# A graph network on one core: SyncE fetches single rows beside GpSimd's gathers

## The chip, the cores and the metric

The kernel runs on one core of a Trainium2 chip. The metric is the device time of one execution in microseconds (us); the median of ten runs stands for the kernel. One execution was also recorded by the hardware profiler, and its trace gives the start and duration of each instruction on TensorE (PE, with its weight loads as PEld), VectorE (DVE), ScalarE (ACT), GpSimd (POOL) and SyncE (SP). What only a sequencer does, such as issuing a DMA, is listed under the engine's name with a q (SPq) and is not counted as busy.

## The reference

Two layers of message passing over a graph of 12,500 nodes with 32 features and 200,000 edges. The edges are sorted by target.

```
h = relu(layernorm(x))
x = x + (sum over edges of h[src] / norms, by dst) @ W + b          # first layer
h = relu(layernorm(x))
# second layer: i = dst, j = src
msg = concat(h[i], h[j] - h[i])                                     # 64 values for each edge
m = relu(relu(relu(msg @ W1 + b1) @ W2 + b2) @ W3 + b3) @ W4 + b4
x = x + (sum of m by dst) / max(count, 1)
```

The product with W1 is split by nodes: one table, tab_i, holds what a target adds to the first hidden layer, and another, tab_j, what a source adds. Both have a row for each node. tab_j is float32 with 64 values (256 bytes) a row, and row number + 48 belongs to a node (OFF = 48).

## The kernel before

A tile is 128 edges, a chunk is 4 tiles (TPC), and a pair is two chunks, 1,024 edges. There are 391 chunks and 196 pairs (NPAIR). The first part of the kernel, up to about 1260 us, computes degrees and the first layer and writes tab_i and tab_j to DRAM, block by block. The last blocks of tab_j and tab_i are written at about 1275 us.

The second layer is one loop over the pairs, written out in full with a schedule by hand: each engine executes its instructions in the order in which the loop issues them. In iteration m of the loop stand

- gather_in(m): the source rows of pair m. For each of the eight tiles GpSimd issues one indirect DMA (helper gather, line 210) that reads 128 row numbers from src_j in SBUF and fetches 128 rows of tab_j into the tile gj. gj has six buffers.
- prepare(m + 3): SyncE issues two DMAs, ai (the rows of tab_i for the pair's targets, line 1003, five buffers) and row (each edge's target relative to its window, spread over the partitions, line 1006, four buffers).
- the stages of earlier pairs, on TensorE with ScalarE and VectorE behind it: fourth(m-6), flip(m-5), third(m-4), second(m-3), first(m-1). first (lines 1022 to 1039) transposes gj into PSUM and adds the product of ai with a one-hot matrix; second and third are the products with W2 and W3 (1047, 1059); flip transposes back (1068), and VectorE copies the result to SBUF (1070); fourth sums messages by target (1079).
- turn(m + 1): VectorE makes the one-hot matrix turned from row (line 1012).

A tiny product with ident_b at the start of first (line 1027) is where TensorE waits for the gathers of a pair. At the end of the program SyncE and the other engines load one flag (bad_i, line 1138) into a register, and a fallback runs only if it is set; here it is not.

Each DMA that SyncE issues signals one of eight semaphores in turn, and waits that the DMA eight before it, which had the same semaphore, has landed.

Of the kernel before, what the change touches and what calls it, by code (L numbers as in the profile page):

```python
# [8 lines left out]
F32 = mybir.dt.float32  # L9
# [7 lines left out]
P = 128  # L17
# [3 lines left out]
HID = 64  # L21
# [4 lines left out]
OFF = 48  # L26
# [5 lines left out]
NPAD = NBLK * P  # L32

TPC = 4
CHUNK = TPC * P
NCH = -(-N_EDGES // CHUNK)
NTR = -(-N_EDGES // P)
# [46 lines left out]
DPAD = (DIR + NDG * GD) * CHUNK  # L84

PC = 32

NROW = NPAD + P

# [2 lines left out]
def gnn_kernel(  # L92
# [20 lines left out]
    nc = tc.nc  # L113
# [17 lines left out]
    tab_j = dram.tile([NPAD, HID], F32, name="tab_j")  # L131
# [9 lines left out]
    def parts(rows):  # L141

        return rows.rearrange("(p j) c -> p j c", p=NPART)
# [25 lines left out]
    xp = fp.tile([NPART, P, D], F32, name="xp")  # L169
    pieces = [slice(j, j + PC) for j in range(0, P, PC)]  # L170
    for at in pieces:
# [37 lines left out]
    def gather(tile_ap, table, col):  # L209
        nc.gpsimd.indirect_dma_start(  # L210
            out=tile_ap, out_offset=None, in_=table,
            in_offset=bass.IndirectOffsetOnAxis(ap=col, axis=0))
# [9 lines left out]
    o = 1 + D  # L222
# [32 lines left out]
    for i, at in enumerate(pieces):  # L255
        h, a = hx[:, at, :D], xp[:, at, :]
        m = fp.tile([NPART, PC], F32, name="la_m", bufs=2)
        nc.vector.tensor_reduce(m, a, AX.X, OP.add)
        nc.vector.tensor_scalar(m, m, 1.0 / D, None, op0=OP.mult)
        nc.vector.tensor_sub(h, a, m[:, :, None].to_broadcast([NPART, PC, D]))  # L260
        nc.vector.tensor_mul(a, h, h)
        v = fp.tile([NPART, PC], F32, name="la_v", bufs=2)
        nc.vector.tensor_reduce(v, a, AX.X, OP.add)
        nc.vector.tensor_scalar(v, v, 1.0 / D, EPS, op0=OP.mult, op1=OP.add)
        sd = fp.tile([NPART, PC], F32, name="la_sd", bufs=2)
        nc.scalar.activation(sd, v, AF.Sqrt)
        nc.vector.reciprocal(v, sd)
        nc.vector.scalar_tensor_tensor(
            h, h, 0.0, v[:, :, None].to_broadcast([NPART, PC, D]), op0=OP.max, op1=OP.mult)
        nc.sync.dma_start(parts(tab_h[OFF:, :])[:, at, :], hx[:, at, :])  # L270
# [2 lines left out]
    first.close()  # L273
    src_j = stay.tile([P, NT], I32, name="src_j")

    def gather_chunk(rows, table, g):
        for t in range(min(TPC, NTR - g * TPC)):
            c = g * TPC + t
            gather(rows[:, t, :], table, src_j[:, c : c + 1])

# [4 lines left out]
    o = dst.offset + DIR * CHUNK  # L285
# [8 lines left out]
    with tc.tile_pool(name="deg", bufs=3) as hp, tc.tile_pool(  # L294
        name="deg_ps", bufs=1, space=bass.MemoryType.PSUM
# [164 lines left out]
        for m, b in enumerate(batches):  # L460
# [4 lines left out]
            if to > gathered:  # L465
                c = slice(gathered * TPC, to * TPC)
                nc.vector.tensor_scalar(src_j[:, c], src_i[:, c], OFF, None, op0=OP.add)
                for g in range(gathered, to):
                    rows = early.tile([P, TPC, D + 1], F32, name="rows_early", bufs=6)
# [9 lines left out]
            for t in range(b, end):  # L479
                g, i = divmod(t - b, HT)  # L480
# [197 lines left out]
    def advance(running):  # L678

        for r in list(running):  # L680
            if next(r, running) is running:
                running.remove(r)
# [7 lines left out]
    NPAIR = -(-NCH // 2)  # L690
    live = {}

    def halves(m):
        return [k for k in range(2) if 2 * m + k < NCH]
# [4 lines left out]
    with tc.tile_pool(name="e0", bufs=8) as sp, tc.tile_pool(name="nu", bufs=1) as np_, tc.tile_pool(  # L699
        name="direct", bufs=1) as dp, tc.tile_pool(name="e0_ps", bufs=1, space=bass.MemoryType.PSUM) as pp, tc.tile_pool(  # L700
        name="nu_ps", bufs=1, space=bass.MemoryType.PSUM) as np_ps:
# [119 lines left out]
        table = dp.tile([P, PART * D3 + P - D3], BF16, name="table")  # L821
# [94 lines left out]
        for m in range(EARLY, DIR + LAG + 1):  # L916
            if m < DIR:
                rows_of[m] = sp.tile([P, TPC, D3], BF16, name="rows")
                gather_chunk(rows_of[m], tab_hn[:, :], m)
# [12 lines left out]
            for slot in slots:  # L932
# [7 lines left out]
                if slot % LATER == 0:  # L940
                    advance(running)
                    later, r = divmod(slot // LATER, NEXT)
# [19 lines left out]
    with tc.manual_schedule(), tc.tile_pool(name="prep", bufs=3) as prep, tc.tile_pool(name="e1", bufs=3) as ep, tc.tile_pool(name="fn", bufs=2) as fp, tc.tile_pool(  # L962
        name="p1_ps", bufs=2, space=bass.MemoryType.PSUM
# [8 lines left out]
        def finish_nodes(q):  # L972

            n = min(J, NBLK - J * q)
            at = slice(J * q, J * q + n)
            c = fp.tile([P, J], F32, name="fn_c")[:, :n]
            nc.vector.tensor_scalar(c, cnt[:, at], 1.0, None, op0=OP.max)
            r = fp.tile([P, J], F32, name="fn_r")[:, :n]
            nc.vector.reciprocal(r, c)
            some = fp.tile([P, J], F32, name="fn_some")[:, :n]  # L980
            nc.vector.tensor_scalar(some, cnt[:, at], 1.0, None, op0=OP.min)
            z = fp.tile([P, J, D], F32, name="fn_z")[:, :n]
            nc.vector.tensor_mul(
                z, b4s[:, None, :].to_broadcast([P, n, D]), some[:, :, None].to_broadcast([P, n, D]))
            nc.vector.tensor_add(z, z, x1[:, at, :])
            yield
            po = message[:, :n]
            for j in range(n):
                nc.tensor.matmul(po[:, j, :], sums.block(J * q + j), w4s, start=True, stop=True)  # L989
            yield  # L990
            y = fp.tile([P, J, D], F32, name="fn_y")[:, :n]
            nc.vector.tensor_mul(y, po, r[:, :, None].to_broadcast([P, n, D]))  # L992
            nc.vector.tensor_add(y, y, z)
            r0 = P * J * q
            nc.sync.dma_start(blocks(out[r0 : r0 + P * n, :]), y)

        def prepare(m):

            v = live[m] = {}
            n, g = len(halves(m)), 2 * m  # L1000
            ai = v["ai"] = prep.tile([P, 2, 3 * HID], BF16, name="ai", bufs=5)
            w = 3 * HID
            nc.sync.dma_start(ai[:, :n], bass.AP(
                tensor=tab_i.tensor, offset=tab_i.offset + STEP * g * w, ap=[[w, P], [STEP * w, n], [1, w]]))
            row = v["row"] = prep.tile([P, 2, CHUNK], F16, name="row", bufs=4)
            nc.sync.dma_start(row[:, :n], bass.AP(
                tensor=rel_row.tensor, offset=rel_row.offset + g * CHUNK, ap=[[0, P], [CHUNK, n], [1, CHUNK]]))

        def turn(m):
            v, n = live[m], len(halves(m))  # L1010
            turned = v["turned"] = prep.tile([P, 2, CHUNK], BF16, name="turned", bufs=3)
            nc.vector.tensor_scalar(turned[:, :n], v["row"][:, :n], part_s, None, op0=OP.is_equal)

        def gather_in(m):
            gj = live[m]["gj"] = ep.tile([P, TPC, 2, HID], F32, name="gj", bufs=6)
            if len(halves(m)) < 2 or (2 * m + 2) * TPC > NTR:
                nc.vector.memset(gj, 0.0)
            for k in halves(m):
                g = 2 * m + k
                gather_chunk(gj[:, :, k, :], tab_j[:, :], g)  # L1020

        def first(m):
            v = live[m]
# [72 lines left out]
        for m in range(AHEAD + 1):  # L1096
            prepare(m)
        turn(0)

        LAST = NPAIR - 1  # L1100
        ENDING = 22
        SHORTER = {second: (12,), third: (20, 10), flip: (18, 8), fourth: (21, 14, 7)}
# [4 lines left out]
        for m in range(NPAIR):  # L1107
            for stage, lag in zip(stages, (1, 3, 4, 5, 6)):
                lag -= len([back for back in SHORTER.get(stage, ()) if LAST - m < back])
                todo[m + lag].append((m, stage))  # L1110
        for now in todo[LAST - ENDING :]:
            now.sort(key=lambda job: (rank(job[1]), job[0]))
        todo[LAST + 1 :] = [[
            (LAST - 2, flip), (LAST - 1, second), (LAST, first), (LAST - 1, third), (LAST - 2, fourth), (LAST, second),
            (LAST - 1, flip), (LAST, third), (LAST - 1, fourth), (LAST, flip), (LAST, fourth)]]
        for m, now in enumerate(todo):
            if m < NPAIR:
                gather_in(m)
            if m == 0:
                for lane in ending:  # L1120
                    assert next(lane, lane) is lane
            if m == LAST:
                ready[NQ - 1] = finish_nodes(NQ - 1)
                next(ready[NQ - 1])
            if m + AHEAD + 1 < NPAIR:
                prepare(m + AHEAD + 1)
            advance(running)
            for k, stage in now:
                stage(k)
                if stage is fourth and (k % (GRP // 2) == GRP // 2 - 1 or k == LAST):  # L1130
                    add_messages(k // (GRP // 2))
            if m + 1 < NPAIR:
                turn(m + 1)
# [5 lines left out]
    with tc.If(bad > 0):  # L1139
        sums0 = dram.tile([NROW, D + 1], F32, name="sums0")  # L1140
        sums1 = dram.tile([NROW, D], F32, name="sums1")
        with tc.tile_pool(name="gp", bufs=1) as gp, tc.tile_pool(name="ge", bufs=1) as ge, tc.tile_pool(
            name="ge_ps", bufs=1, space=bass.MemoryType.PSUM
# [11 lines left out]
            spare = gp.tile([P, 1], F32, name="spare")  # L1155
# [37 lines left out]
            with tc.For_i(0, NTR, 1) as i:  # L1193
                s, d, same, r = edges(i)
                rows = ge.tile([P, D3], BF16, name="g_rows")
# [12 lines left out]
            for q in range(NQ):  # L1208
                n = min(J, NBLK - J * q)
                part = ge.tile([P, J, D + 1], F32, name="g_part")  # L1210
# [9 lines left out]
            with tc.For_i(0, NTR, 1) as i:  # L1220
                s, d, same, r = edges(i)
                gi = ge.tile([P, 3 * HID], BF16, name="g_gi")
                gather(gi, tab_i[:, :], d)
                gj = ge.tile([P, HID], F32, name="g_gj")
# [29 lines left out]
            c = gp.tile([P, NBLK], F32, name="g_c")  # L1254
# [39 lines left out]
```

## Time and profile before

| | |
|---|---|
| median of 10 runs | 3263.04 us (3261.81 to 3267.4) |
| the profiled execution's own time | 3262.19 us |
| its span in the profile | 3260.3 us |
| GpSimd busy | 2443.2 us (75%), of which gathers of gj 1484.6 us (1,563 instructions) |
| TensorE busy | 2539.5 us (78%) |
| VectorE, ScalarE busy | 1554.9 us (48%), 1531.6 us (47%) |
| first and last row of the second layer's gathers | 1277.0 and 3232.7 us |
| granted clock of TensorE | 0.867 on average, 0.82 in the second layer (2000 to 2500 us) |

The span runs from the first to the last instruction that the profiler saw; the device time holds some 1.9 us more. The second layer takes the last three fifths of the span. In rows of instruction groups the numbers after the bar are the busy time in us and the mean of one instruction in ns, and after the second bar the engine's idle time just before these instructions, with what ended it.

### The profile page before, as it was taken

What the parts mean: (1) busy time and instruction counts of PE and PEld (TensorE: products, weight loads), DVE (VectorE), ACT (ScalarE), POOL (GpSimd) and SP (SyncE); (2) the same over time, 40 slices, a digit from 0 to 9 for tenths busy, and PEclk for the clock granted to TensorE, in tenths of its full rate; (3) what the DMA queues carried; (4) which work ended last, traced back from release to release, by engine and by line L of the source; (5) the groups of instructions that cost most, each with busy time, mean ns of one, the idle gap of its engine ahead of it and who ended that gap; (6) DMA issues with size and microseconds to landing.
All of it is one profiled execution on the core that took longest, in us unless ns stands there. A gap on an engine that the chain in (4) does not pass through costs nothing. (4 is left out here: it accounts for less than half of the span.)

```text
span 3260.3 us, 45387 instructions
## 1 busy us (share of the span) xinstructions
PE 2539.5 (78%) x15791; PEld 1614.6 (50%) x15791; DVE 1554.9 (48%) x4067; ACT 1531.6 (47%) x3647; POOL 2443.2 (75%) x2529
## 2 busy tenths in 40 slices
PE   3777999889998995777777777777777777777776
PEld 2664667666666774344434444444444444444333
DVE  8997877777777874222222222222222222222233
ACT  4887888788887882222222222222222222222232
POOL 7777777777776775777777777777777777777775
PEclk8688999999999996788888888888888888888998
DMA  5114121111121112222222222222222222222221
GB/s 110 33 28 94 28 40 35 34 39 33 38 41 36 33 34 66 63 63 63 63 63 63 66 65 63 63 63 63 63 63 63 66 62 65 63 63 63 63 66 31
DMA packets 242764, 180.29 MB, mean 55 GB/s; under 512 B 155496, under 2 KB 191016, under 8 KB 242528
## 3 DMA queue, kind: packets, MB, share of 16 engines
q0 software_dynamic: 80224, 73.28, 12.5%
q1 hardware_dynamic: 157436, 100.80, 11.3%
q10 hardware_dynamic: 4868, 3.23, 0.6%
q8 instruction: 128, 2.10, 0.3%
q14 instruction: 108, 0.88, 0.1%
HBM read 159.32 MB, written 17.78 MB: 54 GB/s over the span
## 5 line engine op out<-in xcount | busy, mean ns | idle before, releaser
L210 POOL DMA_INDIRECT gj<-tab_j,src_j x1563 | 1484.6, 950 | 495.0 <-issue 416.0
L210 POOL DMA_INDIRECT rows<-tab_hn,src_j x752 | 760.9, 1012 | 238.3 <-issue 161.5
L901 ACT ACTIVATE count<-count 128x396 bf16<-128x396 f32 x1857 | 772.9, 513 | 117.2 <-PE count L899 110.2
L899 PE MATMUL count<-oh,lo 128*128 128x396 bf16 x1857 | 483.9, 333 | 68.8 <-DMA rows_early<-tab_h,src_j 24.4
L1079 PE MATMUL ps<-hot,h 128*128 128x256 f32 x1566 | 533.1, 499 | 1.8 <-ACT acc L660 1.2
L1070 DVE COPY h<-p 128x512 f32<-128x512 f32 x196 | 135.4, 691 | 795.5 <-PE p L1068 793.2
L1079 PEld LDWEIGHTS ps<-hot,h 128*128 128x128 f32 x1566 | 379.0, 255 | 183.0 <-issue 104.1
L1038 ACT ACTIVATE h<-p 128x512 f32<-128x512 f32 x196 | 117.0, 597 | 680.7 <-PE p L1034 680.7
L1027 PE MATMUL p<-gj,ident_b 128*1 128x8 bf16 x196 | 34.2, 174 | 486.0 <-DMA gj<-tab_j,src_j 470.9
L845 PE MATMUL st<-count,table 128*128 128x192 bf16 (+1 forms) x3822 | 393.1, 246 | 2.8 <-DVE acc_d L658 2.7
L845 PEld LDWEIGHTS <-table 128*128 128x128 bf16 x3822 | 321.0, 98 | 66.4 <-issue 24.5
L835 DVE TENSOR_SCALAR oh<-number,key 128x1176 bf16<-128x1176 f16 x619 | 318.4, 535 | 70.6 <-PE count L899 69.3
L1061 ACT ACTIVATE h3t<-p,b3c 128x512 f32<-128x512 f32 x196 | 134.7, 687 | 422.2 <-PE p L1059 422.1
L662 DVE TENSOR_TENSOR acc<-acc,ps 64x64 f32<-64x64 f32 (+1 forms) x198 | 44.7, 226 | 603.7 <-PE ps L1079 563.3
L1027 PEld LDWEIGHTS <-ident_b 128*1 128x1 bf16 x196 | 15.5, 79 | 632.8 <-issue 632.5
L1049 ACT ACTIVATE h<-p,b2s 128x1024 f32<-128x1024 f32 x196 | 217.8, 1111 | 118.4 <-PE p L1047 118.4
L686 DVE TENSOR_TENSOR hot<-rel_h,kept 128x512 f32<-128x512 f16 x391 | 250.0, 681 | 2.3
L899 PEld LDWEIGHTS <-lo 128*128 128x128 bf16 x1857 | 174.5, 99 | 152.8 <-issue 100.2
L1034 PE MATMUL p<-turned,ai 128*64 128x512 bf16 x1173 | 235.1, 524 | 0.0
L1047 PE MATMUL p<-h,w2s 64*128 64x512 f32 x782 | 226.1, 654 | 1.3 <-ACT h L1049 1.3
L1059 PE MATMUL p<-h,w3s 128*64 128x512 f32 x782 | 220.1, 641 | 1.8 <-ACT h3t L1061 1.6
L210 POOL DMA_INDIRECT rows_early<-tab_h,src_j x160 | 156.4, 977 | 48.8 <-issue 40.8
(256 smaller groups left out, 2861.8 us busy)
## 6 DMA issues: line engine op xcount, KB each, us to landing
row<-rel_row SPq DMA_DIRECT2D x195, 256.0 KB
gj<-tab_j,src_j POOLq DMA_INDIRECT x1563
ai<-tab_i SPq DMA_DIRECT2D x195, 96.0 KB
rows<-tab_hn,src_j POOLq DMA_INDIRECT x752
srow<-hi_row SPq DMA_DIRECT2D x48, 98.0 KB
tab_i<-nu_terms SPq DMA_DIRECT2D x23, 192.0 KB
rows_back<-tab_early SPq DMA_DIRECT2D x48, 66.0 KB
tab_j<-nu_aij SPq DMA_DIRECT2D x23, 128.0 KB
```

The source lines that it names most:

```text
L210: nc.gpsimd.indirect_dma_start(out=tile_ap, out_offset=None, in_=table, in_offset=bass.IndirectOffsetOnAxis(ap=col, axis=0))
L686: nc.vector.tensor_tensor(hot, rel_h[:, g * TPC : (g + 1) * TPC][:, :, None].to_broadcast([P, TPC, W]), lanes_f[:, None, :W].to_broadcast( ...
L835: nc.vector.tensor_scalar(oh, column, key[:, i : i + 1], None, op0=OP.is_equal)
L845: nc.tensor.matmul(ps[:, : tiles * WD], table[:, h * D3 : h * D3 + P], c[:, :tiles, h, :], start=(h == 0), stop=(h == PART - 1))
L899: nc.tensor.matmul(ps[:, :w], lo[:, i % TPC // 2, :, i % 2], oh[:, a * WD : b * WD], start=True, stop=True)
L901: nc.scalar.activation(counts[g][:, t, a:b, :].rearrange("p h d -> p (h d)"), ps[:, :w], AF.Copy)
L1034: nc.tensor.matmul(p1[k * HID : (k + 1) * HID].rearrange("p t e -> p (t e)"), v["ai"][:, k, i * HID : (i + 1) * HID], v["turned"][:, k], s ...
L1047: nc.tensor.matmul(p2[:, k], w2s[s, :], v["h1"][s, :], start=True, stop=True)
L1049: nc.scalar.activation(h2[:, :n], p2[:, :n], AF.Relu, bias=b2s)
L1059: nc.tensor.matmul(p3[k * HID : (k + 1) * HID], w3s, v["h2"][:, k], start=True, stop=True)
L1070: nc.vector.tensor_copy(h3[:, :, :rows], p4[:, :, :rows])
L1079: nc.tensor.matmul(both[: n * HID, :n, o : o + W], v["h3"][:, t, : n * HID], v["hot"][:, t, :n], start=(i == 0 and t == 0), stop=(last and ...
```

## The change

In the second layer one tile of every eighth pair, 23 tiles in all, is no longer gathered by GpSimd. SyncE fetches its 128 rows one by one into a tile of its own, spare, and VectorE copies that into gj. The rows are spread over the eight iterations ahead of the pair: in each of them SyncE loads 16 source numbers from DRAM into its registers and issues 16 DMAs of one row each, whose source addresses it computes from the registers. This happens in iterations 0 to 183, right after prepare. The last tile of the pair's second chunk is the one that moves. GpSimd has 1,540 gathers of gj instead of 1,563; SyncE has 2,944 more DMAs, 2,944 register instructions for their addresses, and 368 loads into registers (184 for the address of src, 184 for 16 numbers each) with 184 additions; VectorE has 23 more copies, each of which waits for the last eight row fetches.

```diff
+ROWS = 16
+EVERY = P // ROWS
...
-    def gather_chunk(rows, table, g):
-        for t in range(min(TPC, NTR - g * TPC)):
+    def gather_chunk(rows, table, g, n=TPC):
+        for t in range(min(n, NTR - g * TPC)):
             c = g * TPC + t
             gather(rows[:, t, :], table, src_j[:, c : c + 1])
...
         def prepare(m):
 
-            v = live[m] = {}
+            v = live.setdefault(m, {})
...
             for k in halves(m):
                 g = 2 * m + k
-                gather_chunk(gj[:, :, k, :], tab_j[:, :], g)
+                gather_chunk(gj[:, :, k, :], tab_j[:, :], g, TPC - (k == 1 and m in fetched))
+            if m in fetched:
+                nc.vector.tensor_copy(gj[:, TPC - 1, 1, :], live[m].pop("spare"))
+
+        def fetch_rows(m, part):
+
+            v = live.setdefault(m, {})
+            if part == 0:
+                v["spare"] = prep.tile([P, HID], F32, name="spare", bufs=2)
+            o = ((2 * m + 2) * TPC - 1) * P + part * ROWS
+            _, numbers = nc.values_load_multi_w_load_instructions(
+                src[o : o + ROWS].rearrange("(o c) -> o c", o=1), [mybir.EngineType.SP], min_val=0,
+                max_val=NPAD - OFF - 1, skip_runtime_bounds_check_because="numbers of nodes")
+            for k, number in enumerate(numbers):
+                r = part * ROWS + k
+                nc.sync.dma_start(v["spare"][r : r + 1, :], tab_j[bass.ds(number + OFF, 1), :])
...
+        fetched = range(EVERY, NPAIR - EVERY, EVERY)
         LAST = NPAIR - 1
...
             if m + AHEAD + 1 < NPAIR:
                 prepare(m + AHEAD + 1)
+            if m - m % EVERY + EVERY in fetched:
+                fetch_rows(m - m % EVERY + EVERY, m % EVERY)
             advance(running)
```

## The prediction

> **What bounds the kernel now.** I read the page's groups first, then GpSimd's timeline in the second layer, then SyncE's waits and timeline, because the change takes work from the one engine and gives it to the other. In the groups (busy, mean ns | idle before it):
>
> ```profile
> L210 POOL DMA_INDIRECT gj<-tab_j,src_j x1563 | 1484.6, 950 | 495.0 <-issue 416.0
> L1027 PE MATMUL p<-gj,ident_b 128*1 128x8 bf16 x196 | 34.2, 174 | 486.0 <-DMA gj<-tab_j,src_j 470.9
> ```
>
> GpSimd's gathers for the second layer take 1484.6 us, and the idle time between them is mostly "issue", so it waits for nobody. TensorE does wait: 470.9 us until a gather's rows land. GpSimd's timeline in the middle of the stage:
>
> ```profile
> 2012.66 0.94 POOL L210 DMA_INDIRECT gj<-tab_j,src_j  x1 [0.30 <-issue]
> 2013.91 0.94 POOL L210 DMA_INDIRECT gj<-tab_j,src_j  x1 [0.30 <-issue]
> ...
> 2021.59 0.94 POOL L210 DMA_INDIRECT gj<-tab_j,src_j  x1 [0.30 <-DMA gj<-tab_j,src_j]
> 2022.84 0.94 POOL L210 DMA_INDIRECT gj<-tab_j,src_j  x1 [0.30 <-issue]
> ```
>
> One gather follows the other after 1.25 us; the window from 2000 to 2500 us holds 398 of them, 1.256 us each with the odd longer one. A pair of chunks needs eight, so a pair takes 10.05 us. SyncE in the same stretch:
>
> ```profile
> 2012.77 0.36 SPq L1003 DMA_DIRECT2D ai<-tab_i  x1
> 2013.22 0.42 SPq L1006 DMA_DIRECT2D row<-rel_row  x1
> 2022.82 0.36 SPq L1003 DMA_DIRECT2D ai<-tab_i  x1
> 2023.27 0.42 SPq L1006 DMA_DIRECT2D row<-rel_row  x1
> ```
>
> It issues two transfers a pair, and its waits say that the rest is waiting for TensorE to free a buffer of ai:
>
> ```profile
> SPq L1003 <- PE p L1034: 1721.7, 191, 12.0
> ```
>
> So SyncE has about 9 us free in each pair's 10.05. The question is whether 16 fetched rows fit into them.
>
> **What is removed.** fetched holds the pairs 8, 16, ... 184: 23 of them. Each loses one of its eight gathers. As long as GpSimd sets the pace, that is worth 23 x 1.256 = 28.9 us. Nothing more is to be had here: without that much GpSimd still has 7 or 8 gathers a pair, 8.8 to 10.05 us, against TensorE's 381 busy us in 500, 7.6 us a pair.
>
> **What is added on SyncE.** In each of 184 steps (m = 0 to 183) it loads an address, adds to it, loads 16 numbers into registers, and then for each of 16 rows computes an address in registers and issues a DMA of 256 bytes. These stand in the queue behind the ai and row transfers of pair m+3 and ahead of those of pair m+4. SyncE has register work of that kind in one place before, where it reads the flag that guards the fallback (the answer for line 1138):
>
> ```profile
> L1138 SPq TENSOR_LOAD <-bad_i x1: 520/520/520, 157.4 to 157.4; - x1
> L1138 SPq FUSED_REGOPS  x1: 186/186/186, 158.0 to 158.0; - x1
> L1138 SPq SEQ_ASSERT  x1: 33/33/33, 158.2 to 158.2; - x1
> ```
>
> The costs of one step from these rows; between two instructions of SyncE I count 0.05 us:
>
> - ai and row, as now: SyncE's timeline at the start of the layer has ai at 1277.52, row at 1278.03, the next ai at 1278.54, so 1.0 us.
> - The load of the address: 0.52 + 0.07 (the start of the next instruction) = 0.59.
> - The addition: at most a fused register instruction, 0.19 + 0.05 = 0.24; at least the gap alone, 0.05.
> - The load of 16 numbers: no row has more than one number. At the least it costs what one costs, 0.59; at the most every number is a trip of its own, 16 x 0.52 = 8.3. I take the geometric mean, 2.2, since the row can be all overhead or all trip.
> - 16 rows: each a fused register instruction (0.19 + 0.05) and a DMA issue. A row's issue is nearest to the lightest repeated one, ai's median of 0.36, + 0.05. 16 x 0.65 = 10.3. Bounds: with the shortest issue of SyncE's timeline, 0.30 for tab_h at 12.88 us, 16 x 0.59 = 9.4; with the longest of the back-to-back ones at the layer's start, row's 0.47, and its gap, 16 x 0.76 = 12.1.
>
> Sum: 1.0 + 0.59 + 0.24 + 2.2 + 10.3 = 14.3 us a step, from 11.6 with every lower bound (1.0 + 0.59 + 0.05 + 0.59 + 9.4) to 22.2 with every upper one (1.0 + 0.59 + 0.24 + 8.3 + 12.1). All of it is above the 10.05 that GpSimd needs. Even the issues alone, without the loads, come to 11.3.
>
> The Trainium skill's "Runtime: NRT & Kernel Launch", section "Instruction fetch mechanics", puts a load into sequencer registers at about 200 ns a register even in bulk; no row here has a bulk load to confirm it. By it the 16 numbers cost 3.2 us by estimate, the step 15.3 and the kernel some 184 us more than my sum.
>
> The same skill's "DMA: Bandwidth & Descriptors", section "Issuing engine by pattern", calls transfers issued from sync or scalar generally faster and those from GpSimd more flexible, and gives indirect ones to GpSimd. The rows here part the two halves: GpSimd spends 1256 ns on 128 rows, 9.8 ns a row, and SyncE 650 ns on one. By the first half alone one would expect the gain of 28.9 us; by the rows, the second half decides.
>
> **What becomes late.** SyncE's steps are in series, so ai of pair m+4 cannot be issued before step m's rows are. ai has five buffers and row four, a reserve of some three pairs that is used up once; from then on first() of each pair waits for its ai. Every eighth pair has a second wait: VectorE copies spare into gj after the last fetched row has landed, and behind that copy stand flip's copy of h3, the one-hot tiles of third and the next turned, for which TensorE waits in turn. Its place is the same pace: the last part is issued in the step before the copy. GpSimd cannot run on either; gj has six buffers, which first() frees. So the whole stage goes at SyncE's pace for 184 steps, and the 28.9 us saved on GpSimd are lost in its new idle time.
>
> The copies themselves (23 of 128x64 on VectorE) are nearest to the 64x64 addition at 0.23 us, 5 us in all, on an engine that is busy 136 us of 500: nothing. If that cover were gone they would cost those 5 us. Each fetch also waits for the DMA eight before it. The longest landing I can bound is the last store's, issued at 3254.95 and followed by SyncE's next semaphore instruction at 3258.1, so 3.1 us; eight rows take 8 x 0.65 = 5.2, so this adds nothing, and would add only if a landing took longer than that.
>
> **The sum.** Step 0's rows begin at 1278.5 us, when row(3) has been issued. After 184 steps pair 184 can be copied, and pairs 183 to 195 remain. In the profile of before ai(187), which is issued when pair 182's first() ends, is at 3117.45 us, and the end 142.9 us later; 13 x 10.05 = 131 of that are gathers' pace and 12 are the drain. After the change GpSimd is up to six pairs ahead by then, so the rest goes at TensorE's pace: 13 x 7.6 + 12 = 111, and I take 115. Span: 1278.5 + 184 x 14.3 + 115 = 4024.7. The execution took 3262.19 against a span of 3260.3, 1.9 more, and the median 3263.04 is another 0.85 more: 4027 us.
>
> The point from which SyncE decides: 1278.5 + 184 S + 115 = 3260.3 gives S = 10.15 us.
>
> **The rivals.**
>
> *SyncE's step fits (faster).* If the fused instruction costs near to nothing in a row of equal ones (SyncE's assertion next to it took 0.03) and the loads are short, a step is 1.0 + 0.59 + 0.05 + 0.59 + 16 x (0.08 + 0.41) = 10.1, just at the limit; with a lighter issue for a single row it falls below, and GpSimd sets the pace again: 3263.0 - 28.9 = 3234 us. For it: a row is one descriptor, and 186 ns is a single reading. Against it: that reading, and 0.36 of 196 ai issues. 0.08. Between the two, at 10.0 to 10.2, lies no change: 0.01.
>
> *Sixteen trips for sixteen numbers (much slower).* Same mechanism, with the load near its upper bound and the issues near theirs: S = 18.5 to 22.2, so 4800 to 5480 us. 0.08.
>
> *A DMA of one row is slow to issue.* SyncE's only one in the timeline, w1s<-in_b, took 1.73 us where others in the same place of their group took 0.89 to 0.93. With 1.73 + 0.05 a row, S = 1.0 + 0.59 + 0.24 + 2.2 + 16 x 2.02 = 36.4 and the time 8094 us. Against it: ScalarE was issuing a transfer of many 4-byte pieces at that moment. 0.03.
>
> My forecast, SyncE sets the pace with S from 11.6 to 18.5, has the remaining 0.80: 1278.5 + 184 x 11.6 + 115 + 2.8 = 3531, and with 18.5 4800. That is the range too; what it leaves out is the 0.20 of the other cases. Faster by more than 0.2% (what a measurement here can tell from no change): 0.08; within it: 0.01; slower: 0.91.
>
> **What would show it.** Right: SyncE's issues of spare without pauses for TensorE, in groups of 16 and about 0.65 us apart; the wait of ai for p gone; GpSimd and TensorE idle, TensorE before line 1034 or its weights; ai's issues 14 us apart until step 183, about 10 or less after it. The load of 16 numbers in the answer for its line settles the widest term. Wrong: ai still waiting for TensorE with the rows done, and gathers 1.25 us apart throughout; or issues of spare far apart because each waits for a landing.

## The result and the profile after

| | kernel before | changed kernel |
|---|---|---|
| median, same chip | 3264.36 us (28 runs) | 3515.23 us (8 runs, 3510.4 to 3522.74) |
| ratio | | 1.077, 95% interval 1.076 to 1.0779 |
| span of the profiled execution | 3260.3 us | 3512.5 us |
| GpSimd busy, 2000 to 2500 us | 378.84 us, 398 instructions | 321.83 us, 339 instructions |
| TensorE busy, 2000 to 2500 us | 381.09 us | 284.31 us |
| granted clock of TensorE, 2000 to 2500 us | 0.82 | 0.77 |

The kernel is 7.7% slower. The forecast was 4027 us, 512 us too long, and the time lies 16 us below the lower end of the range, 3531 us. The direction and the engine were right; the length of SyncE's step was not. Three of the experiments below (e8, e9 and e10) were measured on a chip on which the kernel before itself took 3982.97 us, against 3264 to 3268 us in the other sets, so their ratios are compared with no others.

The groups of the page first (busy and mean ns, then the idle time before them and what ended it); the first two lines are of the kernel before, in which VectorE and TensorE hardly waited at these places, the other four of the changed kernel:

```profile
L1079 PE MATMUL ps<-hot,h 128*128 128x256 f32 x1566 | 533.1, 499 | 1.8 <-ACT acc L660 1.2
L1012 DVE TENSOR_SCALAR turned<-row,part_s 128x1024 bf16<-128x1024 f16 x196 | 96.9, 495 | 31.0 <-PE p L1034 31.0
...
L213 POOL DMA_INDIRECT gj<-tab_j,src_j x1540 | 1460.7, 949 | 769.1 <-issue 431.7
L1097 PE MATMUL ps<-hot,h 128*128 128x256 f32 x1566 | 468.5, 451 | 792.2 <-DVE h L1088 790.9
L1015 DVE TENSOR_SCALAR turned<-row,part_s 128x1024 bf16<-128x1024 f16 x196 | 98.8, 505 | 505.2 <-DMA row<-rel_row 474.3
L1025 DVE COPY gj<-spare 128x64 f32<-128x64 f32 x23 | 4.8, 210 | 713.0 <-DMA spare<-tab_j 681.1
```

A gather takes as long as before (949 ns), but GpSimd's idle time in front of the gathers has grown from 495.0 to 769.1 us, and "issue" no longer explains it: 1.4 to 3.4 ms into the span GpSimd waits for TensorE to free a gj, 247.5 us in all (total in us, times, longest):

```profile
POOL gj L213 <- PE p L1047: 247.5, 21, 15.9
```

TensorE has new idle time in fourth (line 1097), where it waits for VectorE; and VectorE waits for two things that SyncE issues, row (474.3 us) and spare (681.1 us). Three engines wait in a chain, and at its end is SyncE. The chain of work that ended last names it as well:

```profile
SPq 30%; PE 21%; issue 9%; DVE 3%; DMA 2%; POOL 2%; ACT 2%; DVEq 0%; ACTq 0%; POOLq 0%
```

SyncE's wait for TensorE at ai, 1721.7 us before, is nearly gone (ai is line 1006 here):

```profile
SPq L1006 <- PE p L1052: 53.7, 15, 11.5
```

Its timeline (start, duration, instruction; 16 issues of one step are one row here) has ai 11.5 us apart, and no pause between the rows of a step:

```profile
2001.33 6.97 SPq L1038 DMA_DIRECT2D spare<-tab_j  x16
2008.40 0.40 SPq L1006 DMA_DIRECT2D ai<-tab_i  x1
2008.89 0.42 SPq L1009 DMA_DIRECT2D row<-rel_row  x1
2012.56 6.64 SPq L1038 DMA_DIRECT2D spare<-tab_j  x16
```

From 2009.31, where row is issued, to 2012.56 nothing is in this list: that is the load of the address, the addition, the load of 16 numbers and the first row's address. The profile of lines 1033 and 1038 has these and the rows' parts (minimum, median and maximum in ns, then the first and the last start in us):

```profile
L1033 SPq TENSOR_LOAD <-in_src_ptr x184: 1020/1112/2578, 1278.7 to 3387.7; - x184
L1033 SPq ALU_OP  x184: 41/43/59, 1279.8 to 3388.8; - x184
L1033 SPq TENSOR_LOAD <-in_src x184: 1864/1909/2544, 1279.9 to 3388.9; - x184
...
L1038 SPq FUSED_REGOPS  x2944: 46/46/56, 1282.2 to 3397.7; - x197
L1038 SPq MOVE spare<-tab_j x2944: 29/29/38, 1282.4 to 3397.8; - x197
L1038 SPq DMA_DIRECT2D spare<-tab_j x2944: 224/228/319, 1282.5 to 3397.8; - x197
```

Each row takes two register instructions, FUSED_REGOPS and MOVE, where the section on the change counts one. First and last start give the step: (3387.7 - 1278.7) / 183 = 11.52 us. It consists of 3.48 us until the first row (the two loads and the addition with their gaps), 6.90 us for 16 rows, 0.43 us each, and 1.15 us for ai, row and now and then an output (means of the 183 steps). The last row ends at 3398.1, the span 114.4 us later. So 1278.7 + 184 x 11.52 + 114 = 3512.

### The profile page after: what moved, and what is told of

Its sections match the earlier page's. It is cut to its first block, busy times and chain, and to the rows that moved or that the text cites. A ratio compares the mean times of both kernels' runs of the same rounds, so it can differ in the third digit from the quotient of the medians.

```text
span 3512.5 us, 54955 instructions
## 1 busy us (share of the span) xinstructions
PE 2362.9 (67%) x15791; PEld 1529.6 (44%) x15791; DVE 1564.0 (45%) x4090; ACT 1527.1 (43%) x3647; POOL 2418.4 (69%) x2506
## 3 DMA queue, kind: packets, MB, share of 16 engines
q0 software_dynamic: 79488, 72.52, 11.3%
## 4 chain that ended last, share of the span: by engine, by line
SPq 30%; PE 21%; issue 9%; DVE 3%; DMA 2%; POOL 2%; ACT 2%; DVEq 0%; ACTq 0%; POOLq 0%
SPq L1038 16%; SPq L1033 11%; PE ps L1097 8%; PE p L1065 3%; PE p L1077 3%; PE p L1052 2%; PE p L1086 2%; POOL gj L213 2%; SPq L1009 1%; PE p L1047 1%; SPq L1006 1%; DMA row<-rel_row 1%; ACT count L904 1%; PE st L848 1%; DVE h L1088 1%
## 5 line engine op out<-in xcount | busy, mean ns | idle before, releaser
L213 POOL DMA_INDIRECT gj<-tab_j,src_j x1540 | 1460.7, 949 | 769.1 <-issue 431.7
L1097 PE MATMUL ps<-hot,h 128*128 128x256 f32 x1566 | 468.5, 451 | 792.2 <-DVE h L1088 790.9
L1097 PEld LDWEIGHTS ps<-hot,h 128*128 128x128 f32 x1566 | 331.5, 223 | 926.9 <-DVE h L1088 700.3
L663 ACT ACTIVATE acc<-ps 64x128 f32<-64x128 f32 (+2 forms) x230 | 52.7, 247 | 1073.3 <-DVE acc L665 1073.3
L1015 DVE TENSOR_SCALAR turned<-row,part_s 128x1024 bf16<-128x1024 f16 x196 | 98.8, 505 | 505.2 <-DMA row<-rel_row 474.3
L1025 DVE COPY gj<-spare 128x64 f32<-128x64 f32 x23 | 4.8, 210 | 713.0 <-DMA spare<-tab_j 681.1
L1086 PE MATMUL p<-ident,h3t 128*128 128x128 f32 (+1 forms) x784 | 134.1, 299 | 80.3 <-ACT h3t L1079 47.0
```

Source lines behind the costliest of these rows:

```text
L213: nc.gpsimd.indirect_dma_start(out=tile_ap, out_offset=None, in_=table, in_offset=bass.IndirectOffsetOnAxis(ap=col, axis=0))
L1097: nc.tensor.matmul(both[: n * HID, :n, o : o + W], v["h3"][:, t, : n * HID], v["hot"][:, t, :n], start=(i == 0 and t == 0), stop=(last and ...
```

## The experiments

Two theories could account for the result. *Theory S*: SyncE's instructions are in series, and their sum sets the pace of every pair through ai and row. *Theory V*: the copy of spare sets it; VectorE stands in front of it until the last fetched row has landed, and everything behind it on VectorE is late. The 681.1 us in front of the copy speak for V, the 474.3 us in front of turned for S.

**Only the saving.** e1 leaves the fetches out and clears the tile's place in gj.

```diff
             if m in fetched:
-                nc.vector.tensor_copy(gj[:, TPC - 1, 1, :], live[m].pop("spare"))
+                nc.vector.memset(gj[:, TPC - 1, 1, :], 0.0)
...
-            if m - m % EVERY + EVERY in fetched:
-                fetch_rows(m - m % EVERY + EVERY, m % EVERY)
```

> The 23 tiles are neither gathered nor fetched; VectorE sets their place in gj to zero, so their source rows are left out of the result. It prices the removal alone. If GpSimd sets the pace of the layer before, 23 x 1.256 = 28.9 us go: 3264 - 29 = 3235 us. If TensorE were as near to the limit as its 76% busy time might suggest, less goes, 10 us or so, and gathers show pauses for TensorE.

Measured: 3234.76 us against 3266.49 of the kernel before, ratio 0.9902 (0.9888 to 0.9917). The 23 gathers are worth 32 us (27 to 37 by the interval) when nothing is done in their place, so the saving is there to be had; the changed kernel spends it and 250 us more.

**Only the cost on SyncE.** e2 keeps every fetch, lets GpSimd gather all eight tiles, and drops the copy. Nothing waits for spare.

```diff
-                gather_chunk(gj[:, :, k, :], tab_j[:, :], g, TPC - (k == 1 and m in fetched))
-            if m in fetched:
-                nc.vector.tensor_copy(gj[:, TPC - 1, 1, :], live[m].pop("spare"))
+                gather_chunk(gj[:, :, k, :], tab_j[:, :], g)
```

> SyncE fetches as in the change, but GpSimd gathers all eight tiles of each pair and nothing is copied: the fetched rows are not used, and VectorE waits for none of them. Theory S (SyncE's step of 11.52 us makes ai and row late, whatever waits for the rows): 1278.7 + 184 x 11.5 = 3395 us for the last step, then the nine pairs whose ai is issued after it, at 7.6 us of TensorE each, and 12 us of drain: about 3480 us; VectorE's idle time before turned, for row, grows from the 474 us it had, and gathers wait for TensorE. Theory V (what holds the layer is VectorE's in-order wait for spare, 681 us of its idle time in the changed kernel; the buffers of ai and row would have covered the rest): 3264 us, as before the change.

Measured: 3501.62 us, ratio 1.0721 (1.0705 to 1.0737), against about 3480 us expected; the step is 11.55 us. Its loads of the address (line 1031 there) and two of its waits between 1300 and 3480 us (total, times, longest):

```profile
L1031 SPq TENSOR_LOAD <-in_src_ptr x184: 1033/1119/2413, 1282.1 to 3396.5; - x184
...
DVE turned L1015 <- DMA row<-rel_row: 1465.0, 175, 10.4
...
POOL gj L213 <- PE p L1045: 234.1, 84, 8.1
```

Without the copy, VectorE's wait for row takes the place of both (1465.0 us, against 474.3 for row and 681.1 for spare in the changed kernel), and the pace is the same. Theory V falls: the copy moves the waiting from one instruction to another. In neither kernel does the profile put a wait down to ai; of the two transfers that come late, row is the one that is waited for. The two kernels differ at the end: after the last row 92.8 us remain in e2 and 114.4 us in the changed kernel, and e2 is 14 us shorter in all.

**Rows without loads.** e3 loads 16 numbers once, for all steps (the 23 tiles therefore hold other rows than they should). The 2,944 issues, their landings and the copies remain.

```diff
-            _, numbers = nc.values_load_multi_w_load_instructions(
+            if not numbers:
+                numbers.extend(nc.values_load_multi_w_load_instructions(
...
```

> The 16 numbers are loaded once, in step 0, and all later steps fetch those same rows, so 23 tiles get wrong rows; 2,944 issues, copies and waits stay, 183 of the two loads and the addition go. Theory S: a step loses the 3.48 us from its first load to its first row and takes 6.90 + 1.15 = 8.05 us, which is below 9.9, so GpSimd sets the pace and the removal is earned: about 3237 us. If the rows are what SyncE cannot keep up with, for their landings or their effect on other transfers, it stays above 3264 us.

Measured: 3234.35 us, ratio 0.9905 (0.9891 to 0.992), the time of e1 again. Its waits and its timeline on SyncE:

```profile
SPq L1006 <- PE p L1053: 404.4, 178, 11.5
```

```profile
2004.40 6.59 SPq L1039 DMA_DIRECT2D spare<-tab_j  x16
2013.48 0.39 SPq L1006 DMA_DIRECT2D ai<-tab_i  x1
...
2014.59 6.65 SPq L1039 DMA_DIRECT2D spare<-tab_j  x16
```

ai waits for TensorE again, and between the end of a step's rows (2010.99) and the next ai there are 2.5 us, nearly all of it this wait. So the rows, their landings beside GpSimd's gathers and the copies cost nothing as long as the step fits. The 3.48 us of loading are the whole difference between 0.9% faster and 7.7% slower. (e3 also fetches the same 16 rows in every step; e5 below, which fetches the right ones, agrees with it.)

**Half the rows a step.** e4 fetches 8 rows in each step, for every sixteenth pair, 11 tiles.

```diff
-ROWS = 16
+ROWS = 8
```

> ROWS = 8, so 16 steps for a tile and every sixteenth pair, 11 tiles in all. Theory S: a step takes 3.48 + 8 x 0.43 + 1.15 = 8.1 us, below GpSimd's 10.05, so SyncE keeps up and 11 x 1.256 = 13.8 us are earned: 3250 us. If the wait of VectorE for spare or the loads cost something of their own in each step, the gain is smaller or gone (each microsecond a step costs 176 us, each a tile 11 us).

Measured: 3250.72 us, ratio 0.9959 (0.9946 to 0.9971). ai waits for TensorE 607.9 us in all, and the load of 8 numbers has its price:

```profile
SPq L1006 <- PE p L1052: 607.9, 191, 12.3
```

```profile
L1033 SPq TENSOR_LOAD <-in_src x176: 1062/1096/1755, 1278.5 to 3015.4; - x176
```

8 numbers take 1.10 us and 16 take 1.91: by these two points, 0.10 us a number and 0.28 us besides.

**Twice the loads.** To lengthen the step and nothing else, e10 called the load in a loop of two; the registers of the first load were never read, the program that ran held 184 loads as the changed kernel does, and so nothing was doubled. e11 reads even rows from one load and odd rows from the other.

```diff
-            _, numbers = nc.values_load_multi_w_load_instructions(
+            twice = [nc.values_load_multi_w_load_instructions(
...
-                nc.sync.dma_start(v["spare"][r : r + 1, :], tab_j[bass.ds(number + OFF, 1), :])
+                nc.sync.dma_start(v["spare"][r : r + 1, :], tab_j[bass.ds(twice[k % 2][k] + OFF, 1), :])
```

> The change with each step's loads done twice: two loads of the address, two additions, two loads of the same 16 numbers; the rows are fetched once. Theory S: a step is 11.52 + 3.3 = 14.8 us, and the time 1278.7 + 184 x 14.8 + 117 = 4119 us, 604 more than the change. If the change's loss came from something that a step does once (the landings of its rows, VectorE's wait), the second loads would cost less than their own length: under 3800 us.

> The change with each step's loads done twice, the even rows addressed from the first load and the odd ones from the second, so that both are needed. Theory S: a step is 11.52 + 1.1 + 0.1 + 1.95 + 0.1 = 14.75 us, and the time 1278.7 + 184 x 14.75 + 117 = 4110 us, some 595 more than the change. If the change's loss came from something that a step does once (the landings of its rows, VectorE's wait), the second loads would cost less than their own length: under 3800 us.

Measured for e10: 4822.71 us, ratio 1.2129 (1.206 to 1.2197), in the set of 3982.97 us, which says nothing on the question. Measured for e11: 4081.68 us, ratio 1.2505 (1.2482 to 1.2528), where 4110 us were expected. Its loads of the address, two a step:

```profile
L1033 SPq TENSOR_LOAD <-in_src_ptr x368: 982/1028/2344, 1281.1 to 3956.1; - x184
```

The step is 14.60 us, 3.08 more than in the changed kernel, and 184 x 3.08 = 567 us are the 566 by which the time grew. Theory S holds in proportion, not only in sign.

**Numbers from SBUF.** If the loads decide, cheaper loads must turn the result. e5 brings the 128 numbers of a tile to SBUF by one DMA, a tile ahead, and loads 16 registers from there; the load of the address is gone too.

```diff
+        def number_row(m):
+
+            v = live.setdefault(m, {})
+            v["numbers"] = prep.tile([1, P], I32, name="numbers", bufs=3)
+            o = ((2 * m + 2) * TPC - 1) * P
+            nc.sync.dma_start(v["numbers"], src[o : o + P].rearrange("(o c) -> o c", o=1))
...
-                src[o : o + ROWS].rearrange("(o c) -> o c", o=1), [mybir.EngineType.SP], min_val=0,
+                v["numbers"][:, o : min(P, o + ROWS)], [mybir.EngineType.SP], min_val=0,
```

> One DMA a tile brings the 128 numbers into one partition of SBUF, and SyncE loads 16 of them a step from there; the load of the address and the addition go, the rest is as in the change. Loads from DRAM took 1.10 us for 8 numbers and 1.91 for 16, 0.10 a number and 0.28; the flag from SBUF took 0.52 for one number, so 16 should take about 2.0 us. Theory S: a step takes 2.0 + 0.1 + 6.90 + 1.15 = 10.15 us, just over GpSimd's 9.9: 1278.7 + 184 x 10.15 + 117 = 3263 us, within 20 us of the kernel before; at 1.6 us for the load it would fall under 9.9 and earn nearly all of 28.9 us: 3237. If the loads overlapped with the issues in some way, taking half of them off would change nothing: 3515 us.

Measured: 3238.71 us against 3268.27, ratio 0.9904 (0.9888 to 0.9919): 1% faster than the kernel before, with all 23 tiles fetched by SyncE. The expected 3263 us were missed because the load took 1.17 us and not 2.0:

```profile
L1042 SPq TENSOR_LOAD <-numbers x184: 1142/1167/1242, 1287.3 to 3090.2; - x184
```

```profile
SPq L1006 <- PE p L1061: 171.1, 111, 11.5
```

SyncE's work in a step is now 1.23 (the load and its gap) + 6.89 (rows) + 1.15 = 9.3 us. The steps still come only every 9.85 us, the rest being waits, and 9.85 is about GpSimd's pace with one gather in 64 gone: 10.05 x 63/64 = 9.89.

**How many rows are best.** e7 is e5 with 15 rows a step (20 tiles), e6 with 11 (15 tiles).

```diff
-ROWS = 16
-EVERY = P // ROWS
+ROWS = 15
+EVERY = -(-P // ROWS)
```

> As e5, with 15 rows a step and every ninth pair, 20 tiles. Theory S: a step takes 1.9 + 0.1 + 15 x 0.43 + 1.15 = 9.6 us, under the 9.91 that GpSimd needs with 71 gathers in nine pairs, so 20 x 1.256 = 25.1 us are earned: 3264 - 25 = 3239 us. If a step has hidden waits once SyncE is nearly full (ai late now and then), it gives back some of it: 3245 to 3264.

> As e5, with 11 rows a step and every twelfth pair, 15 tiles. Theory S: 1.5 + 0.1 + 11 x 0.43 + 1.15 = 7.5 us a step, with 2.4 us of SyncE free, so 15 x 1.256 = 18.8 us are earned: 3245 us. It has the reserve that e7 lacks; if e7 is not 6 us faster than this, the last of SyncE's time is not to be had.

Measured: 3240.33 us, ratio 0.9911 (0.9896 to 0.9926), and 3247.39 us, 0.9931 (0.9917 to 0.9944). Per tile that SyncE takes over, e5, e7 and e6 gain 1.3 to 1.4 us, about one gather's pitch, so the gain goes by the number of tiles and SyncE's room is worth nothing beyond fitting. The loads of both became longer than e5's, and e7's step, with a row less than e5's, is not lighter but heavier: from its first load to its last it is 10.01 us on average, with next to no wait in it. That is 0.1 us above the 9.91 that GpSimd needs, and the gain is still there; over 180 steps the lag adds up to 18 us, less than two pairs, which the buffers can presumably take up. e6's and e7's loads:

```profile
L1042 SPq TENSOR_LOAD <-numbers x180: 1337/2460/2505, 1283.4 to 3056.6; - x180
```

```profile
L1042 SPq TENSOR_LOAD <-numbers x180: 705/3262/3305, 1279.2 to 3071.0; - x180
```

15 numbers at 3.26 us against 16 at 1.17. In e5 each load starts at a multiple of 64 bytes in the tile, in e7 at a multiple of 60. Single loads of e7, of the fourth and the fifth step of a tile (byte 180 and byte 240):

```profile
L1042 SPq TENSOR_LOAD <-numbers x1: 3261/3261/3261, 2028.2 to 2028.2; - x1
```

```profile
L1042 SPq TENSOR_LOAD <-numbers x1: 1589/1589/1589, 2039.1 to 2039.1; - x1
```

Byte 240 is a multiple of 16 and byte 180 is not; the tile's first step, byte 0, has 1.64 and 1.62 us at 1997.4 and 2087.1. e6 has the same division: 2.46 us for 11 numbers, and 1.35 to 1.42 us in every fourth step, whose start is a multiple of 16 bytes. To have every start on such a boundary, e8 gives each step's 15 numbers a row of 16:

```diff
+            v["numbers"] = prep.tile([1, EVERY, 16], I32, name="numbers", bufs=3)
```

> As e7, but each step's 15 numbers start at a multiple of 64 bytes in SBUF. In e7 most loads of 15 numbers took 3.26 us where e5's of 16 took 1.17; those of e7 that started at a multiple of 16 bytes took 1.6. If the start of the load makes the difference, all loads here take about 1.6 us and a step 9.3; if the number of values makes it, they stay at 3.26. The time should not tell: 20 tiles, 3240 us as e7, since GpSimd sets the pace in both or nearly; e7's steps averaged 10.0 us against the 9.91 that GpSimd needs, so 0 to 15 us less than e7.

Measured: 4517.49 us, ratio 1.1357 (1.1309 to 1.1406), in the set of 3982.97 us. On that chip the kernel is 13.6% slower than the kernel before; its trace shows SyncE pausing between one instruction of a step and the next, mostly for 0.6 to 0.8 us. The gaps of more than 0.15 us add up to 757 us from 1700 to 4300 us, where e7 has 23 us of them from 1300 to 3050 us, and a step takes 14.8 us. Why SyncE pauses there was not found, so the time decides nothing on the loads. The duration of the load does:

```profile
L1041 SPq TENSOR_LOAD <-numbers x180: 3/1562/1935, 1663.8 to 4317.9; - x180
```

Its median is 1.56 us, half of e7's, even on that chip. The start is not all, though: from an equally good start e5's 16 numbers took 1.17 us, less than 15 here. What the count does was not followed up.

**A second engine.** e9 and e12 are one kernel in two sets: 22 rows a step and 31 tiles, of which SyncE fetches 16 rows and ScalarE 6.

```diff
-ROWS = 16
+ROWS = 22
+SYNC = 16
...
+            for queue, engine, at in (
+                (nc.sync, mybir.EngineType.SP, range(0, SYNC)), (nc.scalar, mybir.EngineType.Activation, range(SYNC, n))):
```

> Numbers in SBUF as in e8, 22 rows a step and every sixth pair, 31 tiles; SyncE fetches 16 rows of a step and ScalarE the other 6. Theory S: SyncE's step stays at e5's 9.2 us of work, GpSimd needs 47 gathers in six pairs, 9.84 us a pair, ScalarE gets 0.7 + 6 x 0.42 = 3.2 us a pair on top of 2.7: 31 x 1.256 = 38.9 us earned, 3226 us. If ScalarE's loads and issues, which stand in its queue ahead of the activations that TensorE waits for, lengthen TensorE's chain beyond the pair's 9.84 us, or if its issues wait for SyncE's through the eight shared semaphores, it is slower than e5's 3239 us.

> Numbers in SBUF, each step's at a multiple of 16 bytes, 22 rows a step and every sixth pair, 31 tiles; SyncE fetches 16 rows of a step and ScalarE the other 6. Theory S: SyncE's step stays at e5's 9.2 us of work, GpSimd needs 47 gathers in six pairs, 9.84 us a pair, ScalarE gets 0.7 + 6 x 0.42 = 3.2 us a pair on top of 2.7: 31 x 1.256 = 38.9 us earned, 3226 us. If ScalarE's loads and issues, which stand in its queue ahead of the activations that TensorE waits for, lengthen TensorE's chain beyond the pair's 9.84 us, or if its issues wait for SyncE's through the eight shared semaphores, it is slower than e5's 3239 us.

Measured for e9: 1.2301 (1.2261 to 1.2342), in the set of 3982.97 us. Measured for e12: 3510.36 us against 3263.93, ratio 1.0758 (1.0743 to 1.0773), slower again, against the 3226 us expected. SyncE has the cheap load of e5 and the same 16 rows, yet its step is 11.46 us. Here are its load and its largest wait in this part of the kernel, one that the changed kernel does not have:

```profile
L1045 SPq TENSOR_LOAD <-numbers x186: 1154/1170/1517, 1281.2 to 3401.3; - x186
...
SPq L1050 <- DMA spare<-tab_j: 291.5, 168, 8.4
```

SyncE waits for landings of spare before it issues the next row. With the smaller waits for landings (33.7 us at ai, 23.8 us at row, and 27.3 us at rows for a landing of row) that is 376 us, 2.0 us in each of 186 steps; without them a step would be 9.4 us. The wait fits the rule by which DMAs take eight semaphores in turn: both engines draw on the same eight, a row of SyncE's that follows one of ScalarE's on a semaphore cannot be issued until that one has landed, and ScalarE issues its rows between its own activations. The trace of e12 bears this out. In it the DMAs of both engines signal the same eight semaphores; after 1300 us, 171 rows of SyncE's that come next after a row of ScalarE's on their semaphore were held up for more than 0.15 us, 287 us in all; in waits that make up 210 us of that, SyncE had begun to wait before ScalarE had even issued its row. A kernel with separate semaphores was not run. ScalarE pays too: ahead of its activations it stands idle for 315.2 us (acc) and 235.8 us (h3t) that the profile puts down to spare, its own issuing of six rows a step (2.45 us) included.

The four kernels whose step lies above GpSimd's pace agree with one sum within 0.6%; the step in it is the measured one, so what this tests is that nothing is left over beside start, steps and end. 1278.7 + 184 S + 114 gives 3512 for the changed kernel (S = 11.52, span 3512.5) and 4079 for e11 (14.60, median 4081.68), and with 92.8 us at the end 3497 for e2 (11.55, span 3499.6); with 186 steps and a start at 1281.2, 3527 for e12 (11.46, span 3508.6).

## Why the prediction was right and wrong

**The mechanism** was right in the main. SyncE sets the pace, ai's wait for TensorE has gone, and GpSimd's and TensorE's waits are the new ones. e2 shows it with nothing but the fetches added, e11 shows that each microsecond of the step returns 184 times. The place of the wait was wrong: first() was to wait for its ai and TensorE to stand idle before the products with ai, but no wait is put down to ai. VectorE waits, for row and spare, and TensorE's new idle time is in fourth, behind VectorE (790.9 us).

**The decision point** of 10.15 us was right as far as the runs go: 9.3 us of work a step (e5) and 10.0 (e7) give the gain, 11.5 (the change, e2 and e12) the loss. No run lies between 10.0 and 11.5.

**The saving** of 28.9 us was nearly right: 32 us in e1, 29.6 us in e5. Both intervals hold 28.9, so the excess over GpSimd's pitch of 1.256 us a gather (1.38 for each in e1, 1.29 in e5) is not clear of noise.

**The start and the tail** were right: 1278.5 and 115 us forecast, 1278.7 and 114.4 measured. The 115 was rounded up from 111, so its fit to within 1 us is luck in part; e2 has 92.8. That the end goes at TensorE's pace fits as well: from 3400 to 3512 us TensorE is busy for 90.2 of 112 us.

**The step of 14.3 us** failed, and in it the term of the 16 rows: 10.3 us forecast, 6.90 measured, below even the lower bound of 9.4. Both parts of it were too dear. The fused register instruction was taken at 186 ns from a single reading beside the fallback's flag, which SyncE reads at 157.4 us and not at the end of the program; in a run of equal ones it takes 46 ns, and the second register instruction of a row, MOVE, for which the sum had no term, takes 29. The issue was taken at 0.36 us from ai, whose transfer is of 96 KB, and its lower bound of 0.30 us from another with many rows; one row of 256 bytes takes 0.228 us. A bound taken from the smallest number in sight was no bound, because nothing in the trace before was as light as the new instruction. The text had the case ("a lighter issue for a single row") but gave it 0.08 together with short loads, and did not move the forecast's own lower end.

**The loads** were too cheap, which hid part of that. Forecast: address 0.59, addition 0.24 at most, 16 numbers 2.2, together 3.03; measured: 1.11, 0.043, 1.91, with gaps 3.48. The geometric mean for the 16 numbers was near; the address, loaded from DRAM, costs twice the flag that stood for it. ai, row and the output take 1.15 for 1.0. The sum of the errors, -3.4 + 0.45 + 0.15 = -2.8 us, times 184 is -515 us, and 4027 - 515 = 3512.

**The claim that the issues alone suffice** ("Even the issues alone, without the loads, come to 11.3") was wrong, and it matters more than the 512 us. Rows, ai and row come to 8.05 us, well inside the pair's 10.05. e3 has just these and is 0.95% faster. So the sign was right for another reason than the one given most weight: it hangs on the loads, and e5 turns it by changing where the numbers are loaded from. With the rows at their measured 6.90 us the forecast's own loads of 3.03 us still give 10.9 us, above 10.15, but only by 0.8 and not by the 4.2 us of the forecast. The first rival, in which the step fits at 10.1 us, was only 1.4 us a step from what was measured; its rows of 0.49 us were still too dear, its loads of 0.59 us too cheap.

**The landings** add nothing, as forecast: in the changed kernel SyncE issues its rows without a pause. That holds while SyncE alone uses the semaphores; in e12 SyncE's waits for earlier landings take 2.0 us a step.

**The page's price of a register load.** The Trainium skill's "Runtime: NRT & Kernel Launch", section "Instruction fetch mechanics", gives about 200 ns a register even in bulk. Here that is so only for loads from SBUF that start off a 16-byte boundary (3.26 us for 15 in e7); from DRAM it was 0.10 us a number and 0.28 us besides, and 16 aligned ones from SBUF took 1.17 us, 73 ns each (e5). The measurements decide: by the page e5 would have had a step of some 11.3 us by estimate and no gain.

**Row against gather.** The Trainium skill's "DMA: Bandwidth & Descriptors", section "Issuing engine by pattern", gives indirect transfers to GpSimd, and the forecast held on to that. At 430 ns a row from SyncE against 9.8 ns from GpSimd it stays true per row; e5, 1% faster than the kernel before, shows that it still pays to let the slow engine do some, when it has idle time and the fast one sets the pace.

## What to carry to other kernels

Before work is given to an idle sequencer, add up its instructions for one step of the loop against the bound engine's pace; here a step that was over by 15% (11.52 against 10.05 us) cost that 15% in every iteration, while those of 9.3 and 10.0 us cost nothing. Here the loads into registers were the first to shorten: bring the numbers to SBUF ahead of time, load them from an aligned start, and avoid loading an address for each step. Where an operation is lighter than anything in the profile, the lightest row there is an upper bound for it, not a lower one.

## What the runs showed of the hardware

- Loads into SyncE's registers: 1.11 us for the address of an input (changed kernel); 8 and 16 numbers from DRAM 1.10 us (e4) and 1.91 us (changed kernel); 16 numbers from SBUF 1.17 us (e5, e12), and 15 from SBUF 1.6 us from a start at a multiple of 16 bytes and 3.26 us from another (e7); 11 take 1.35 to 1.42 and 2.46 us (e6).
- One row of 256 bytes whose address is in a register costs SyncE 46 ns (address) + 29 ns (move) + 228 ns (issue), with gaps 0.43 us (changed kernel); issuing a transfer of 96 KB in 256 rows costs 0.36 us at the median, 0.33 to 0.46 us (ai in the kernel before).
- Two engines that issue DMAs on the same eight semaphores can hold each other up: in steps of 16 rows, which SyncE alone issued without a pause, SyncE waited 2.0 us a step for landings when ScalarE issued six more (e12). That the shared semaphores are the cause is read from the trace and was not tested by a run of its own.
